# A layer norm's last step on VectorE instead of GpSimd, from period 8 of block 0 and in block 1's attention

## The chip, the cores and the metric

The kernel runs on one core of a Trainium2 chip. A core has five engines with a queue each: TensorE (PE in the profile: matrix products and transposes), VectorE (DVE), ScalarE (ACT), GpSimd (POOL) and SyncE (SP, which only starts transfers here). An engine executes its own queue strictly in the order in which it was written; between engines, semaphores order the work. The metric is the time of one execution on the device in microseconds (us). The number that a run is compared by is the median of several executions.

## The reference

There are 32 sequences of 256 tokens with 128 features, 8192 rows of 128 numbers in float32. Two blocks follow each other, each with an attention part and a part of experts.

```python
def _layer(x, ...):                       # block 0's attention part, run twice
    xl = _ln(x, ln1_g, ln1_b)
    q, k, v = ...                         # projections, rotary
    probs = softmax(q k / sqrt(64))
    x = x + att @ wo
    xl2 = _ln(x, ln2_g, ln2_b)
    hid = xl2 @ w1 + b1
    hid = hid * sigmoid(1.702 * hid)
    return x + hid @ w2

def _layernorm(x, axis=-1, eps=1e-05):
    m = jnp.mean(x, axis=axis, keepdims=True)
    v = jnp.var(x, axis=axis, keepdims=True)
    return (x - m) / jnp.sqrt(v + eps)
```

Block 0's experts: a router picks 8 of 64 experts for a token, each expert takes at most 64 tokens, and the weighted results are added to a shared expert's result. Block 1 has linear attention (with a layer norm of its output before the last projection) and 32 experts, one per token, again with a shared one. Layer norms without learned weights stand between the parts.

## The kernel before

**Tiles.** The 8192 rows are 64 tiles of 128 rows; four tiles make a group (`GT = 4`), so there are 16 groups of 512 rows. All rows live in `s_rows` on the chip. A layer norm always handles one group at a time, in `normed` (L103): for each of the four tiles VectorE computes mean and variance (`bn_stats` L109, `bn_aggr` L110, into `bn_mv`). GpSimd then makes 1/sqrt(variance + eps) for the four tiles in two small operations of 128x4, an addition (L111) and a power with −0.5 (L112), negates the mean (L118) and writes the four normalised tiles, `z = (x − mean) * rs`, with one 128x128 operation each (L120). In the form that block 1's attention uses (`on_act`), GpSimd multiplies the mean with the inverse deviation (L114) and VectorE writes the tiles (L116). `bn_mv` and `bn_rs` have three buffers, `z` four.

**Who uses the norm in block 0.** `norm_t` (L355) normalises a group into `z`, has TensorE transpose its four tiles (L127) and ScalarE copy the result to `xt` (L363). `project` (L366) does this ahead of the attention's projections, `second_norm` (L490) ahead of the hidden layer. `enter` (L186), the norm of the input rows, and `route` (L625), that between the blocks, call `normed` in the GpSimd form.

**Periods.** Block 0 runs in 18 periods, the loop at L583. A unit is a pair of groups in one of the two layers; there are 16. Period k runs attention for unit k (`softmax`, L391: scores L403, maxima L409, exponentials L418, transposes L435, products with the values L444, its result copied at L450) and, beside it (`beside`, L537), the second norms and hidden layer of unit k−1, the output layer of unit k−2 and the norms and projections of unit k+1. The hidden layer (`widen`, L476) has four steps a group: a matmul (L480), ScalarE's `m_z` from the result (L482, two buffers), ScalarE's tanh into `m_h` (L484, twelve buffers), and VectorE's product of both, again into `m_h` (L485), which sets the `m_z` buffer free. The output layer (`narrow`, L494) multiplies `m_h` at L498. Matmul results of most steps share two banks (`bank`, L73).

**The experts of block 0.** From period 8 on each period also runs two calls of `experts` (L295), each for four experts: two gathers of rows by index (L303), matmuls, and four scatter-adds of results into `moe0` in device memory (L341), so eight adds in a full period. Gathers and adds are indirect transfers, which GpSimd issues from its own queue. Every add waits for the one before it to have landed, since both add to the same array.

**Order.** The steps of a period are generators that `run` advances in turn. The framework's scheduler turns what they issue into one queue for each engine, before the kernel runs.

**Block 1.** `linear_attention` (L778) handles one group at a time and calls `normed` at L839 in the `on_act` form on `l_o`, in place; what it returns, the last GpSimd operation of the norm, is kept in `last_norm`, and the scatters in `send` (L763) are ordered behind it.

Of the kernel before, what the change touches and what calls it, by code (L numbers as in the profile page):

```python
# [16 lines left out]
F32 = mybir.dt.float32  # L17
# [8 lines left out]
P = 128  # L26
# [34 lines left out]
def recurrent_kernel(ctx: ExitStack, tc: tile.TileContext, x, consts, small0, wsd, wgu, wd, small1, bias1, wr, out):  # L61
# [38 lines left out]
    power = keep.tile([P, GT], F32, name="power")  # L100
    vec.memset(power, -0.5)

    def normed(wk, src, dst, on_act=False):  # L103

        st = wk.tile([P, GT, 6], F32, name="bn_st")
        mv = wk.tile([P, GT, 2], F32, name="bn_mv", bufs=3)
        rs = wk.tile([P, 2, GT], F32, name="bn_rs", bufs=3)
        for j in range(GT):
            vec.bn_stats(st[:, j], src[:, j])  # L109
            vec.bn_aggr(mv[:, j], st[:, j])  # L110
        pool.tensor_scalar(rs[:, 0], mv[:, :, 1], 1.0, EPS, ALU.mult, ALU.add)  # L111
        pool.tensor_tensor(rs[:, 0], rs[:, 0], power, ALU.pow)  # L112
        if on_act:
            ins = pool.tensor_tensor(rs[:, 1], mv[:, :, 0], rs[:, 0], ALU.mult)  # L114
            for j in range(GT):
                vec.tensor_scalar(dst[:, j], src[:, j], rs[:, 0, j : j + 1], rs[:, 1, j : j + 1], ALU.mult, ALU.subtract)  # L116
            return ins
        pool.tensor_scalar(rs[:, 1], mv[:, :, 0], -1.0, 0.0, ALU.mult, ALU.add)  # L118
        for j in range(GT):
            ins = pool.tensor_scalar(dst[:, j], src[:, j], rs[:, 1, j : j + 1], rs[:, 0, j : j + 1], ALU.add, ALU.mult)  # L120
        return ins

    def transposed(src):
# [10 lines left out]
    with ExitStack() as c0:  # L134
# [217 lines left out]
            order_of += [(p, 0), (p - 2, 1)]  # L352
        order_of += [(p, 1) for p in range(NG // 2 - 2, NG // 2)]

        def norm_t(g, copy):  # L355

            xs = s_all[:, g * GT : (g + 1) * GT]
            z = wk.tile([P, GT, D], F32, name="z", bufs=4)
            normed(wk, xs, z)
            yield  # L360
            ps = transposed(z)
            xt = wk.tile([P, GW], F32, tag="xt", name="xt", bufs=4)
            copy(xt, ps)  # L363
            yield xt

        def project(g, l, got):  # L366

            xt = None
            for xt in norm_t(g, act.copy):
                yield  # L370
            w = [par("attn", (4 * l + i) * D, D) for i in range(3)]
            qk = []
            for i, rot in enumerate(("rotq", "rotk")):
                ps = bank()
                pe.matmul(ps, w[i], xt, start=True, stop=True)  # L375
                t = wk.tile([P, GW], F32, name=f"a_qk{i}", bufs=4)
                vec.scalar_tensor_tensor(
                    t.rearrange("p (b s) -> p b s", s=SEQ), ps.rearrange("p (b s) -> p b s", s=SEQ),
                    fold[:, l, i : i + 1], bcast(const(rot), 1, 2), ALU.add, ALU.mult,
                )  # L380
                qk.append(t)
                yield
            ps = bank()
            for j in range(GT):
                pe.matmul(ps[:, j * D : (j + 1) * D], xt[:, j * P : (j + 1) * P], w[2], start=True, stop=True)
            v = wk.tile([P, GT, D], F32, name="a_v", bufs=4)
            act.copy(v, ps.rearrange("p (t d) -> p t d", d=D))
            got[g] = (qk, v)
            yield
# [97 lines left out]
                yield  # L487
            got[g] = hs

        def second_norm(g, got):  # L490
            for got[g] in norm_t(g, act.copy):
                yield

        def narrow(g, l, hs):  # L494
# [28 lines left out]
        def unit(k):  # L523
            p, l = order_of[k]
            return (2 * p, 2 * p + 1), l
# [3 lines left out]
        def first(g):  # L529
            yield from enter(g)  # L530
            if g == 0:
                fold_in()
            yield from project(g, 0, qkv)

        drain(run(*(first(g) for g in unit(0)[0])))

        def beside(k):  # L537

            if 1 <= k <= units:
                yield from run(*(second_norm(g, mid) for g in unit(k - 1)[0]))  # L540
            if 2 <= k:
                gs, l = unit(k - 2)
                yield from run(*(narrow(g, l, wide.pop(g)) for g in gs))
            if 1 <= k <= units:
                gs, l = unit(k - 1)
                yield from run(*(widen(mid.pop(g), l, wide, g) for g in gs))
            if k + 1 < units:
                gs, l = unit(k + 1)
                if gs[0] not in entered:
                    entered.update(gs)  # L550
                    yield from run(*(enter(g) for g in gs))
                yield from run(*(project(g, l, qkv) for g in gs))


        entered = {0, 1}
# [222 lines left out]
    def linear_attention(g):  # L778

        xt = xt_all[:, g * GW : (g + 1) * GW]  # L780
        ps = bank()
        pe.matmul(ps, par1("wq"), xt, start=True, stop=True)
        qf = wk.tile([P, GW], F32, name="l_q")
        act.activation(qf, ps, AF.Silu, bias=par1("bq"))
        q2 = wk.tile([P, GW], F32, name="l_q2", bufs=1)
        act.activation(q2, qf, AF.Square, bias=half)
        vec.tensor_scalar(qf, qf, 0.5, None, ALU.add)
        ps = bank()
        for j in range(GT):
            pe.matmul(ps[:, j * H1 : (j + 1) * H1], q2[:, j * P : (j + 1) * P], const("bones"), start=True, stop=True)  # L790
        norms = wk.tile([P, GT * (1 + O1) * H1], F32, name="l_n")
        qn, kn = norms[:, : GT * H1], norms[:, GT * H1 :]
        vec.tensor_copy(qn, ps[:, : GT * H1])
        yield

        kf = wk.tile([P, GT, O1 * D], F32, name="l_k")
        vf = wk.tile([P, GT, O1 * D], F32, name="l_v")
        for j in range(GT):
            ps = bank("sc", 4)
            pe.matmul(ps, xt[:, j * P : (j + 1) * P], par1("wkv"), start=True, stop=True)  # L800
            vec.tensor_tensor(kf[:, j], ps[:, : O1 * D], bias[:, : O1 * D], ALU.add)
            vec.tensor_tensor(vf[:, j], ps[:, O1 * D :], bias[:, O1 * D : 2 * O1 * D], ALU.add)
            if j % 2:
                yield

        sp.dma_start(xt.rearrange("p (t d) -> p t d", d=D), rows(moe1, g))
        act.activation(kf, kf, AF.Silu)
        k2 = wk.tile([P, GT * O1 * H1, D1], F32, tag="wide", name="l_k2")
        kflat = kf.rearrange("p t (h d) -> p (t h) d", d=D1)
        act.activation(k2, kflat, AF.Square, bias=half)  # L810
        vec.tensor_reduce(kn, k2, AX.X, ALU.add)
        yield
        act.activation(norms, norms, AF.Sqrt)
        vec.tensor_scalar(norms, norms, 1e-6, None, ALU.add)
        vec.reciprocal(norms, norms)  # L815
        vec.scalar_tensor_tensor(kflat, kflat, 0.5, bcast(kn, 2, D1), ALU.add, ALU.mult)
        yield
        ps = bank("tr", 2)
        for b in range(2):
            for k in range(O1):  # L820
                for j in range(2):
                    pe.matmul(  # L822
                        ps[:, (k * 2 + b) * D : (k * 2 + b + 1) * D], kf[:, 2 * b + j, k * D : (k + 1) * D],
                        vf[:, 2 * b + j, k * D : (k + 1) * D], start=j == 0, stop=j == 1,
                    )
        yield
        st4 = ps.rearrange("p (k b d) -> p k b d", b=2, d=D)
        st = wk.tile([P, 2, D], F32, name="l_st")
        vec.tensor_tensor(st, st4[:, 0], bcast(const("bmask"), 1, 2), ALU.mult)
        vec.tensor_tensor(st, st4[:, 1], st, ALU.mult)  # L830
        ps = bank()
        for j in range(GT):
            pe.matmul(ps[:, j * D : (j + 1) * D], qf[:, j * P : (j + 1) * P], st[:, j // 2], start=True, stop=True)
        o = wk.tile([P, GT, D], F32, tag="tok", name="l_o", bufs=3)
        vec.tensor_tensor(
            o.rearrange("p t (h d) -> p (t h) d", d=D1), ps.rearrange("p (n d) -> p n d", d=D1), bcast(qn, 2, D1), ALU.mult
        )
        yield
        last_norm.append(normed(wk, o, o, True))  # L839
        yield  # L840
        ps = transposed(o)
        ot = wk.tile([P, GW], F32, tag="chan", name="l_ot", bufs=3)
        act.activation(ot, ps, AF.Identity, bias=par1("lb"), scale=par1("lg"))
        yield
        ps = bank()
        for j in range(GT):
            pe.matmul(ps[:, j * D : (j + 1) * D], ot[:, j * P : (j + 1) * P], par1("wo"), start=True, stop=True)
        assert len(sent) >= (g + 1) * GT
        vec.tensor_tensor(
            s_all[:, g * GT : (g + 1) * GT], ps.rearrange("p (t d) -> p t d", d=D), bcast(bias[:, 4 * D :], 1, GT), ALU.add  # L850
        )
        yield
# [169 lines left out]
```

## Time and profile before

| what | value |
| --- | --- |
| median of 3 executions | 1429.88 us (1424.03 to 1430.29) |
| the profiled execution's own time | 1431.9 us |
| its span (first to last instruction) | 1430.1 us |
| mean clock granted to TensorE | 0.953 of full speed |
| `z` tiles written by GpSimd, 128x128 (L120) | 256, 504 ns each |
| `l_o` tiles written by VectorE, 128x128 (L116) | 64, 348 ns each |
| L111, L118, L114 on GpSimd, 128x4 | 237, 203, 200 ns each |

How to read the lines that follow: a group's line names the source line, engine, operation, the tile written and the tiles read, then how often it occurred, its busy time, the mean nanoseconds of one, and behind the last bar the idle time of the engine just before these instructions with what ended most of it. A line of the timeline has start and duration in us, engine, source line, operation and tiles, and in brackets a wait before it with what released it; neighbouring instructions of one kind can stand in one line. Durations and waits are of one profiled execution. Instructions that only issue a transfer are listed with the time that the issue took on GpSimd.

### The profile page before, as it was taken

To read this page: it belongs to the slowest core of one execution; us is meant where nothing else is said; L and a number is where in the kernel's file an instruction comes from. 1 tells how busy PE (TensorE), PEld (TensorE's weight loads), DVE (VectorE), ACT (ScalarE), POOL (GpSimd) and SP (SyncE) were. 2 spreads that over 40 slices of the span, in tenths; PEclk is the share of its full clock that TensorE was granted. 3 is DMA by queue.
4 is the path that set the end of the run, shared out by engine and by line. 5 is a ranking of instruction groups with operands and counts; after the bars stand their busy time and mean duration, and the time that the engine had idled before them with its cause. 6 is when DMAs were issued, how large, how long until landed. Compare 5 with 4: busy or idle time off the path is not lost. (4 is left out here: it accounts for less than half of the span.)

```text
span 1430.1 us, 22784 instructions
## 1 busy us (share of the span) xinstructions
PE 1250.7 (87%) x7395; PEld 871.3 (61%) x7395; DVE 920.6 (64%) x2971; ACT 773.1 (54%) x1842; POOL 683.4 (48%) x1100
## 2 busy tenths in 40 slices
PE   6989998899899999999999758899766899999787
PEld 4645665565567656766566435566444777788763
DVE  4689899869956565556454347755655565656437
ACT  1675566566666666566665434444333454645342
POOL 6353437442345665666645407652466444343430
PEclk9989999999999999999999988999787899999999
DMA  5022231210102212221220044211411467666656
GB/s 181 9 56 62 69 97 52 75 33 12 52 12 50 44 15 49 50 44 27 38 51 4 6 108 130 67 38 37 124 55 54 130 190 210 194 197 198 185 174 191
DMA packets 131079, 120.50 MB, mean 84 GB/s; under 512 B 17456, under 2 KB 108432, under 8 KB 130832
## 3 DMA queue, kind: packets, MB, share of 16 engines
q1 hardware_dynamic: 119184, 103.26, 24.8%
q0 software_dynamic: 11776, 15.78, 4.9%
q8 instruction: 59, 0.97, 0.3%
q14 instruction: 60, 0.49, 0.1%
HBM read 81.01 MB, written 37.99 MB: 83 GB/s over the span
## 5 line engine op out<-in xcount | busy, mean ns | idle before, releaser
L895 POOL DMA_INDIRECT back<-e_ys,e_toi x96 | 97.3, 1013 | 141.2 <-ACT e_ys L894 104.4
L418 ACT ACTIVATE a_pr<-ps_sc,a_nm 128x256 f32<-128x256 f32 x256 | 119.5, 480 | 74.5 <-DVE a_nm L409 69.0
L341 POOL DMA_INDIRECT moe<-e_y,sidx x64 | 95.1, 1486 | 128.4 <-DMA moe<-e_y,sidx 71.4
L480 PE MATMUL ps_mm<-xt,sw 128*128 128x512 f32 x256 | 134.5, 629 | 2.8 <-ACT r_ex L215 2.1
L111 POOL TENSOR_SCALAR bn_rs<-bn_mv 128x4 f32<-128x4 f32 x112 | 26.5, 237 | 220.5 <-DVE bn_mv L110 203.5
L120 POOL TENSOR_SCALAR z<-s_rows,bn_rs 128x128 f32<-128x128 f32 x256 | 125.8, 504 | 6.9
L498 PE MATMUL ps_mm<-sw,m_h 128*128 128x128 f32 x1024 | 126.5, 279 | 2.5 <-DVE s_h L250 0.9
L498 PEld LDWEIGHTS ps_mm<-sw,m_h 128*128 128x128 f32 x1024 | 118.5, 192 | 15.2 <-issue 8.2
L485 DVE SCALAR_TENSOR_TENSOR m_h<-m_h,m_z 128x512 f32<-128x512 f32 x128 | 88.2, 696 | 49.0 <-ACT m_h L484 48.4
L112 POOL TENSOR_TENSOR bn_rs<-bn_rs,power 128x4 f32<-128x4 f32 x112 | 114.4, 1022 | 1.3
L482 ACT ACTIVATE m_z<-ps_mm,fold 128x512 f32<-128x512 f32 x128 | 87.0, 688 | 43.8 <-PE ps_mm L480 43.5
L881 PE MATMUL ps_sc<-e_xt,e_w 128*128 128x128 f32 x768 | 101.2, 279 | 3.3 <-ACT e_xt L868 2.2
L409 DVE TENSOR_REDUCE a_nm<-ps_sc 128x2 f32<-128x512 f32 x128 | 83.1, 682 | 32.0 <-PE ps_sc L403 27.8
L881 PEld LDWEIGHTS ps_sc<-e_xt,e_w 128*128 128x128 f32 x768 | 94.7, 195 | 9.5 <-issue 5.8
L403 PE MATMUL ps_sc<-a_qk,a_qk 64*128 64x256 f32 x512 | 95.4, 412 | 1.4 <-ACT a_pr L418 1.2
L484 ACT ACTIVATE m_h<-m_z 128x512 f32<-128x512 f32 x128 | 80.2, 636 | 1.8
L435 PEld LDWEIGHTS ps_tr<-con,a_pr 128*128 128x128 f32 x512 | 59.0, 144 | 32.2 <-issue 20.3
L765 POOL DMA_INDIRECT xslot<-s_rows,dest x64 | 65.0, 1016 | 27.9 <-issue 18.5
L435 PE MATMUL ps_tr<-con,a_pr 128*128 128x128 f32 x512 | 75.1, 281 | 3.3 <-DVE key L236 2.2
L375 PE MATMUL ps_mm<-xt,sw 128*128 128x512 f32 x128 | 74.4, 693 | 3.9 <-ACT xt L363 1.6
L127 PEld LDWEIGHTS ps_tr<-con,z 128*128 128x128 f32 x256 | 33.0, 147 | 73.2 <-POOL z L120 45.5
L127 PE MATMUL ps_tr<-con,z 128*128 128x128 f32 x256 | 51.9, 298 | 28.9 <-POOL z L120 26.3
(225 smaller groups left out, 2982.0 us busy)
## 6 DMA issues: line engine op xcount, KB each, us to landing
e_w<-in_wr_dram SPq DMA_DIRECT2D x96, 384.0 KB
xslot<-zero SPq DMA_DIRECT2D x4, 1548.0 KB
e_x<-xslot SPq DMA_DIRECT2D x24, 258.0 KB
e_wg<-in_wgu_dram SPq DMA_DIRECT2D x16, 384.0 KB
x_in<-in_x_dram SPq DMA_DIRECT2D x16, 256.0 KB
tab<-s_rows SPq DMA_DIRECT2D x16, 256.0 KB
moe<-s_y SPq DMA_DIRECT2D x16, 256.0 KB
c_g<-moe SPq DMA_DIRECT2D x16, 256.0 KB
```

Of the source, the lines that this page charges most:

```text
L112: pool.tensor_tensor(rs[:, 0], rs[:, 0], power, ALU.pow)
L120: ins = pool.tensor_scalar(dst[:, j], src[:, j], rs[:, 1, j : j + 1], rs[:, 0, j : j + 1], ALU.add, ALU.mult)
L341: pool.indirect_dma_start(out=moe0, out_offset=bass.IndirectOffsetOnAxis(ap=sidx[:, 4 * q + e : 4 * q + e + 1], axis=0), in_=ye[:, e], in_ ...
L403: pe.matmul(sc[h][:, j * SEQ : (j + 1) * SEQ], qk[0][hd, q0 : q0 + P], qk[1][hd, b * SEQ : (b + 1) * SEQ], start=True, stop=True,)
L418: act.activation(pr[:, n], sc[h][:, j * SEQ : (j + 1) * SEQ], AF.Exp, bias=nm[:, n : n + 1], accum_out=su[:, n : n + 1],)
L435: pe.transpose(pts[:, n * P : (n + 1) * P], pr[:, n, k * P : (k + 1) * P], ident)
L480: pe.matmul(ps, par("w1", l * FF0 + f * P, P), xt, start=True, stop=True)
L482: act.activation(z, ps, AF.Identity, bias=fold[:, l, 3 + f : 4 + f])
L485: vec.scalar_tensor_tensor(h, h, 1.0, z, ALU.add, ALU.mult)
L498: pe.matmul(ps[:, j * D : (j + 1) * D], hs[f][:, j * P : (j + 1) * P], par("w2", l * FF0 + f * D, D), start=f == 0, stop=f == 3,)
L881: pe.matmul(ps[:, c * P : (c + 1) * P], wt[:, c * P : (c + 1) * P], xt[:, j * P : (j + 1) * P], start=True, stop=True,)
L895: ins = pool.indirect_dma_start(out=back, out_offset=bass.IndirectOffsetOnAxis(ap=toi[:, j : j + 1], axis=0), in_=ys[:, j], in_offset=None,)
```

## The change

`normed` takes the engine that is to write the tiles, `on`. With VectorE, GpSimd computes only the addition and the power, and VectorE writes the four tiles from the mean in `bn_mv` and the inverse deviation in `bn_rs`. That form is used in block 0 by `first` (the two groups ahead of the periods) and, from period 8 on, by the second norms and projections in `beside`; in block 1 by the attention's norm. Periods 0 to 7, `enter` and `route` keep GpSimd's form. The inverse deviation and the negated mean have a tile each, `bn_rs` and `bn_nm`. A form for ScalarE is in the code and is not called.

```diff
-    def normed(wk, src, dst, on_act=False):
+    def normed(wk, src, dst, on=None):
...
-        rs = wk.tile([P, 2, GT], F32, name="bn_rs", bufs=3)
+        rs = wk.tile([P, GT], F32, name="bn_rs", bufs=3)
         for j in range(GT):
             vec.bn_stats(st[:, j], src[:, j])
             vec.bn_aggr(mv[:, j], st[:, j])
-        pool.tensor_scalar(rs[:, 0], mv[:, :, 1], 1.0, EPS, ALU.mult, ALU.add)
-        pool.tensor_tensor(rs[:, 0], rs[:, 0], power, ALU.pow)
-        if on_act:
-            ins = pool.tensor_tensor(rs[:, 1], mv[:, :, 0], rs[:, 0], ALU.mult)
+        pool.tensor_scalar(rs, mv[:, :, 1], 1.0, EPS, ALU.mult, ALU.add)
+        ins = pool.tensor_tensor(rs, rs, power, ALU.pow)
+        if on is vec:
             for j in range(GT):
-                vec.tensor_scalar(dst[:, j], src[:, j], rs[:, 0, j : j + 1], rs[:, 1, j : j + 1], ALU.mult, ALU.subtract)
+                vec.tensor_scalar(dst[:, j], src[:, j], mv[:, j, 0:1], rs[:, j : j + 1], ALU.subtract, ALU.mult)
             return ins
-        pool.tensor_scalar(rs[:, 1], mv[:, :, 0], -1.0, 0.0, ALU.mult, ALU.add)
-        for j in range(GT):
-            ins = pool.tensor_scalar(dst[:, j], src[:, j], rs[:, 1, j : j + 1], rs[:, 0, j : j + 1], ALU.add, ALU.mult)
+        nm = wk.tile([P, GT], F32, name="bn_nm", bufs=3)
+        pool.tensor_scalar(nm, mv[:, :, 0], -1.0, 0.0, ALU.mult, ALU.add)
...
+        for j in range(GT):
+            ins = pool.tensor_scalar(dst[:, j], src[:, j], nm[:, j : j + 1], rs[:, j : j + 1], ALU.add, ALU.mult)
         return ins
...
-            yield from project(g, 0, qkv)
+            yield from project(g, 0, qkv, vec)
...
         def beside(k):
 
+            on = pool if k < 8 else vec
             if 1 <= k <= units:
-                yield from run(*(second_norm(g, mid) for g in unit(k - 1)[0]))
+                yield from run(*(second_norm(g, mid, on) for g in unit(k - 1)[0]))
...
-                yield from run(*(project(g, l, qkv) for g in gs))
+                yield from run(*(project(g, l, qkv, on) for g in gs))
...
-        last_norm.append(normed(wk, o, o, True))
+        last_norm.append(normed(wk, o, o, vec))
```

In the changed kernel line numbers are 5 higher behind the changed function, and 6 higher behind the first lines of `beside`; the new writes on VectorE are at L115.

More of the change, by code (lines that the diff above doesn't have):

```diff
@@ L110, in normed @@
             vec.bn_aggr(mv[:, j], st[:, j])
-        pool.tensor_scalar(rs[:, 0], mv[:, :, 1], 1.0, EPS, ALU.mult, ALU.add)
-        pool.tensor_tensor(rs[:, 0], rs[:, 0], power, ALU.pow)
-        if on_act:
-            ins = pool.tensor_tensor(rs[:, 1], mv[:, :, 0], rs[:, 0], ALU.mult)
+        pool.tensor_scalar(rs, mv[:, :, 1], 1.0, EPS, ALU.mult, ALU.add)
+        ins = pool.tensor_tensor(rs, rs, power, ALU.pow)
+        if on is vec:
             for j in range(GT):
-                vec.tensor_scalar(dst[:, j], src[:, j], rs[:, 0, j : j + 1], rs[:, 1, j : j + 1], ALU.mult, ALU.subtract)
+                vec.tensor_scalar(dst[:, j], src[:, j], mv[:, j, 0:1], rs[:, j : j + 1], ALU.subtract, ALU.mult)
             return ins
-        pool.tensor_scalar(rs[:, 1], mv[:, :, 0], -1.0, 0.0, ALU.mult, ALU.add)
+        nm = wk.tile([P, GT], F32, name="bn_nm", bufs=3)
+        pool.tensor_scalar(nm, mv[:, :, 0], -1.0, 0.0, ALU.mult, ALU.add)
+        if on is act:
+            pool.tensor_tensor(nm, nm, rs, ALU.mult)
+            for j in range(GT):
+                act.activation(dst[:, j], src[:, j], AF.Identity, scale=rs[:, j : j + 1], bias=nm[:, j : j + 1])
+            return ins
         for j in range(GT):
-            ins = pool.tensor_scalar(dst[:, j], src[:, j], rs[:, 1, j : j + 1], rs[:, 0, j : j + 1], ALU.add, ALU.mult)
+            ins = pool.tensor_scalar(dst[:, j], src[:, j], nm[:, j : j + 1], rs[:, j : j + 1], ALU.add, ALU.mult)
         return ins
@@ L353, in recurrent_kernel, with norm_t @@
         order_of += [(p, 1) for p in range(NG // 2 - 2, NG // 2)]
-        def norm_t(g, copy):
+        def norm_t(g, copy, on):
             xs = s_all[:, g * GT : (g + 1) * GT]
             z = wk.tile([P, GT, D], F32, name="z", bufs=4)
-            normed(wk, xs, z)
+            normed(wk, xs, z, on)
             yield
@@ L364, in norm_t, with project @@
             yield xt
-        def project(g, l, got):
+        def project(g, l, got, on):
             xt = None
-            for xt in norm_t(g, act.copy):
+            for xt in norm_t(g, act.copy, on):
                 yield
@@ L488, in widen, with second_norm @@
             got[g] = hs
-        def second_norm(g, got):
-            for got[g] in norm_t(g, act.copy):
+        def second_norm(g, got, on):
+            for got[g] in norm_t(g, act.copy, on):
                 yield
```

## The prediction

> **What bounds the kernel now.** I read the page's table of engines, then its costliest groups, then only the stretch that the change touches: the eight periods from 446 to 824 us in which the experts' results are added (P1 to P8, each from its first scatter-add to the next period's; starts 446.38, 491.64, 539.53, 587.70, 634.65, 679.92, 727.74, 778.32). From the page:
>
> ```profile
> PE 1250.7 (87%) x7395; PEld 871.3 (61%) x7395; DVE 920.6 (64%) x2971; ACT 773.1 (54%) x1842; POOL 683.4 (48%) x1100
> ...
> L341 POOL DMA_INDIRECT moe<-e_y,sidx x64 | 95.1, 1486 | 128.4 <-DMA moe<-e_y,sidx 71.4
> ...
> L120 POOL TENSOR_SCALAR z<-s_rows,bn_rs 128x128 f32<-128x128 f32 x256 | 125.8, 504 | 6.9
> ...
> L112 POOL TENSOR_TENSOR bn_rs<-bn_rs,power 128x4 f32<-128x4 f32 x112 | 114.4, 1022 | 1.3
> ```
>
> TensorE is the bound, GpSimd far from one. Busy time by windows, P3 and P5 (PE, PEld, DVE, ACT, POOL, clock, DMA share, GB/s):
>
> ```profile
> 539.50:587.70 48.20, 45.07 (x286) 30.32 (x288) 27.34 (x81) 30.03 (x79) 29.20 (x41) 0.96 0.20 41
> 634.70:679.90 45.20, 43.37 (x286) 29.62 (x286) 27.44 (x81) 29.90 (x79) 29.25 (x40) 1.00 0.21 42
> ```
>
> TensorE works for 94 to 96% of a period, VectorE and GpSimd for 57 to 65%. So what counts is who holds TensorE up, and in which order GpSimd's and VectorE's queues stand. The timeline of P3:
>
> ```profile
> 556.43 0.30 DVE L110 BATCH_NORM_AGGREGATE bn_mv<-bn_st 128x2 f32<-128x6 f32 x2
> ...
> 556.98 0.69 DVE L485 SCALAR_TENSOR_TENSOR m_h<-m_h,m_z 128x512 f32<-128x512 f32 x1 [0.25 <-ACT m_h L484]
> ...
> 559.84 1.29 ACT L482 ACTIVATE m_z<-ps_mm,fold 128x512 f32<-128x512 f32 x2
> ...
> 560.60 1.08 PE L444 MATMUL ps_mm<-a_pt,a_v 128*64 128x256 f32 x8
> ...
> 563.28 1.40 POOL L341 DMA_INDIRECT moe<-e_y,sidx  x1 [1.79 <-DMA moe<-e_y,sidx]
> ...
> 566.48 1.83 POOL L341 DMA_INDIRECT moe<-e_y,sidx  x1 [1.80 <-DMA moe<-e_y,sidx]
> ...
> 568.38 0.19 POOL L111 TENSOR_SCALAR bn_rs<-bn_mv 128x4 f32<-128x4 f32 x1
> 568.66 0.19 POOL L118 TENSOR_SCALAR bn_rs<-bn_mv 128x4 f32<-128x4 f32 x1
> 568.81 1.04 POOL L112 TENSOR_TENSOR bn_rs<-bn_rs,power 128x4 f32<-128x4 f32 x1
> ...
> 569.96 1.75 POOL L120 TENSOR_SCALAR z<-s_rows,bn_rs 128x128 f32<-128x128 f32 x4
> ...
> 570.47 1.77 PE L127 MATMUL ps_tr<-con,z 128*128 128x128 f32 x4 [2.55 <-POOL z L120]
> ```
>
> To be seen: VectorE has the statistics of the unit's first second norm (call it A; B is its other group, C and D the two groups that project next) at 556.7, but GpSimd starts A at 568.4, because eight scatter-adds stand ahead of it, one every 3.3 us (1.45 to issue, 1.8 for the previous add to land). Nobody but TensorE's transposes needs A, and they lose only 2.55 us; meanwhile VectorE goes on with the hidden activations m_h.
>
> **What the Trainium skill says.** "GPSIMD Engine Reference", § 4.1 Engine selection, gives elementwise work to VectorE. The trace agrees by less than that page's factor two: 504 ns for a 128x128 tile at L120, 348 ns at L116. "TensorE: Matmul & The Clock Gate", Part 1, has TensorE's clock fall after an idle window of about 3.4 us. The trace agrees: after a wait of 7.58 us in P8 eight L444 matmuls take 1.98 us where they take 1.08 in P3. "DMA: Bandwidth & Descriptors", Rules for kernel authors, says that an accumulating DMA has to wait for the earlier one on the same bytes; the 1.8 us at each L341 is that wait, so the chain of adds will not get faster.
>
> **The change part by part.** Off GpSimd: 34 groups lose L118 and four L120 (34 x (0.20 + 4 x 0.504) = 75 us), 16 lose L114 (3 us). Onto VectorE: 34 x 4 writes of 0.348 = 47 us, of which 5.5 in each full period. GpSimd was no bound; the direct gain is only where TensorE waits for z.
>
> *Gain, P1 to P6.* The transposes of A wait for GpSimd's z: 0.85 + 0.53 us in P1, P4 and P5, which with slower transposes (0.77 + 0.76 where an undisturbed four take 0.60) makes 2.3; in P2, P3, P6 2.25, 2.55 and 2.35, transposes 1.1 slower, and about 1.4 of slow matmuls behind, 4.9. All gone: 3 x 2.3 + 3 x 4.9 = 21.6. The periods bear it out: P3 is 3.0 us longer than P5.
>
> *Loss, P1 to P6.* In the order of the changed kernel the queues in such a period stand thus. GpSimd: seven adds (with four gathers between), power of A, eighth add, powers of B, C, D. VectorE: statistics of A, four z of A, then the m_h. Nothing stands between A's last bn_aggr and its first z. VectorE takes its queue in order, so it stands from A's statistics (17.2 us after the period's start) until the power of A: the end of add seven, less 1.0 (one pair of gathers moves behind), plus 1.4 (L111, L112 and gaps). Behind it stand m_h. m_z has two buffers, so the third m_z, 20.3 us after the period's start (559.84 in P3), waits for the first m_h, and with it ScalarE, the two matmul banks, and TensorE's next L444. The third m_z comes at: end of add seven + 0.4 + 0.34 (first z's lead) + 0.69 (one m_h), and add seven ends 23.4, 24.7, 25.1, 23.7, 23.2, 25.2 us after the start. With the remaining three z counted in part, it is late by 4.6, 5.9, 6.4, 4.9, 4.4, 6.4: together 32.6 us. TensorE has nothing else, as its own queue is in order too. Stalls of this length slow what follows: L444 1.98 for 1.08 and L480 1.65 to 1.93 for 1.12 make 1.4 to 1.7 a period where nothing absorbs them; I take 1.4 x 6 = 8.5.
>
> *VectorE's own pace.* 5.5 us of z a period and the waits of B, C, D for a power (1.3 us each less the small operations ahead of them). The work alone is 33 us over six periods, and VectorE has some 20 us free in each, but m_h and the softmax reductions (L409) are what ScalarE waits for. From zero (all in idle time) to 27; I take 14.
>
> *P7.* Six adds stand ahead of the first power (C's, 749.8 now), VectorE reaches it near 741: blocked 9, with slow matmuls behind 11. The stalls that go are 3.01 + 0.85 + 0.53 with slow matmuls behind, 7.3. Net +4. *P8.* All eight adds come first and TensorE already waits 7.58 us there; z comes at most 1.2 earlier: −1. *Block 1.* The wait of L116 for L114 (14.7 us over all) loses a 0.2 us operation 11 times or so: −2. The scatters of block 1 (L765) are ordered behind a group's last GpSimd norm operation, now the power instead of L114: the same place in the queue, nothing. *The two groups ahead of the periods*: eight z written faster by 0.15: −1.
>
> Sum: 32.6 + 8.5 − 21.6 + 14 + 4 − 1 − 2 − 1 = **+33.5 us**. The profiled execution took 1431.9 us with a span of 1430.1; the median, 1429.88, is 0.2 below that span, so I add to the median: **1463**.
>
> **The rivals.** *Faster: the block is not met.* If the power of A were there when VectorE asks, the gains stand alone: 21.6 + 7.3 (P7) + 1 + 2 + 1 = 33, less some pacing, say 5: 1402. For it: before, the same stall cost TensorE little. Against: the adds would have to end some 7 us earlier; it decides at 2.2 us an add instead of 3.3, or if anything but m_h stood behind z. *Even: blocked, but absorbed.* If half of the delay were taken up by buffers (the score banks hold softmax work that needs no m_h) and the pacing were nothing: (32.6 + 8.5) / 2 − 21.6 + 4 − 4 = −1; with some pacing 1429 to 1440. For it: GpSimd's A was 2.55 us late for TensorE, not 8. Against: the third m_z stands on ScalarE's queue ahead of the attention output (L450) and the copies of the next transposes, so all of them wait. *Much slower*: pacing at its 27, restart of slow matmuls at 1.7, B and C adding 1 us a period: 33.5 + 13 + 2 + 6 = +54.5: 1484. For it: bn_aggr and z of B, C, D follow each other with little between; against: 20 us of idle VectorE a period. That the change is not built as it reads is excluded: 136 z stand on VectorE's queue and are gone from GpSimd's.
>
> **How the numbers follow.** Forecast (1445 to 1475): 0.50; much slower: 0.22; even: 0.15; faster: 0.13. Two executions of this kernel differ by up to 0.4%, so under 0.5% (7 us) is no change. Faster by more: all of the faster case and a little of the even one, 0.14. Within: 0.07. Slower: 0.79. The range of 1422 to 1494 leaves out most of the faster case and the far end of the slow one.
>
> **What would show it.** Right: a wait of VectorE at the new z (L115) for the power of L112 of some 6 to 9 us in P1 to P7, 45 to 65 in all; TensorE waiting for ScalarE's m_z at L444 or L480 instead of for z at L127; full periods of 49 to 54 us; GpSimd's busy time down by 78, VectorE's up by 47 us. Wrong: full periods under 46 us with short waits at L115 (faster), or long waits at L115 while TensorE stays above 94% busy (even). A change far from 446 to 824 us would mean that I looked in the wrong place.

## The result and the profile after

The changed kernel takes 1464.57 us (median of 4 executions, 1459.96 to 1471.28) against 1427.01 for the kernel before: a ratio of 1.026, with a 95% interval from 1.0224 to 1.0295. It is slower by 37.6 us; the forecast was 33.5. The profiled execution of the changed kernel took 1459.96 us with a span of 1458.2. It is the fastest of its four executions, while the profiled one of the kernel before, 1431.9 us, is slower than that kernel's median; so the two traces lie only 28.1 us apart.

From the page of the changed kernel, the table of engines and three groups (line numbers are 5 or 6 higher than before):

```profile
PE 1253.0 (86%) x7395; PEld 872.7 (60%) x7395; DVE 949.9 (65%) x3107; ACT 775.0 (53%) x1842; POOL 608.0 (42%) x914
...
L346 POOL DMA_INDIRECT moe<-e_y,sidx x64 | 95.7, 1495 | 130.1 <-DMA moe<-e_y,sidx 62.6
...
L112 POOL TENSOR_TENSOR bn_rs<-bn_rs,power 128x4 f32<-128x4 f32 x112 | 114.1, 1019 | 4.2
...
L115 DVE TENSOR_SCALAR z<-s_rows,bn_mv,bn_rs 128x128 f32<-128x128 f32 x136 | 41.9, 350 | 84.9 <-POOL bn_rs L112 84.8
```

GpSimd lost 75 us of work and VectorE gained 29, with 350 ns for each z where GpSimd needed 504 (neighbouring operations of VectorE overlap, so that four z in a row take 1.12 us). Yet in front of the new z VectorE stood idle for 84.9 us, nearly all of it for the power of L112. The waits between 430 and 870 us (total, number of times, longest), one line of the kernel before, then those of the changed kernel:

```profile
PE ps_tr L127 <- POOL z L120: 25.3, 14, 7.6
...
DVE z L115 <- POOL bn_rs L112: 82.4, 30, 9.5
...
ACT m_z L487 <- DVE m_h L490: 45.3, 13, 8.4
...
PE ps_mm L449 <- ACT m_z L487: 33.3, 6, 6.9
...
PE ps_tr L440 <- DVE a_pr L432: 11.7, 7, 7.0
...
PE ps_tr L132 <- DVE z L115: 8.5, 2, 7.3
```

The lines form a chain: VectorE waits for GpSimd, ScalarE for VectorE, TensorE for ScalarE, six times. The wait of TensorE for z at the transposes, 25.3 us in this stretch before, is gone but for the 8.5 us in two places, both in P8. The same chain in P3, from the timeline of the changed kernel (VectorE has the statistics of A, the first group of the unit's second norms, at 570.1):

```profile
569.85 0.30 DVE L110 BATCH_NORM_AGGREGATE bn_mv<-bn_st 128x2 f32<-128x6 f32 x2
...
576.33 1.40 POOL L346 DMA_INDIRECT moe<-e_y,sidx  x1 [2.73 <-DMA moe<-e_y,sidx]
...
577.79 0.20 POOL L111 TENSOR_SCALAR bn_rs<-bn_mv 128x4 f32<-128x4 f32 x1
578.07 1.04 POOL L112 TENSOR_TENSOR bn_rs<-bn_rs,power 128x4 f32<-128x4 f32 x1
579.15 0.35 DVE L115 TENSOR_SCALAR z<-s_rows,bn_mv,bn_rs 128x128 f32<-128x128 f32 x1 [9.00 <-POOL bn_rs L112]
579.41 0.68 DVE L490 SCALAR_TENSOR_TENSOR m_h<-m_h,m_z 128x512 f32<-128x512 f32 x1
...
580.19 0.69 ACT L487 ACTIVATE m_z<-ps_mm,fold 128x512 f32<-128x512 f32 x1 [6.80 <-DVE m_h L490]
...
580.93 1.97 PE L449 MATMUL ps_mm<-a_pt,a_v 128*64 128x256 f32 x8 [6.94 <-ACT m_z L487]
```

Read it from the bottom up. TensorE's products with the values begin 6.94 us late, because ScalarE has not emptied a bank into m_z; that was 6.80 us late, because both m_z buffers were full until VectorE's first m_h; VectorE stood 9.00 us at z, whose power came after the seventh add. Then the matmuls run slowly, 1.97 us where eight of them took 1.08 before.

Busy time by windows, P3 and P5 of the changed kernel (PE, PEld, DVE, ACT, POOL, clock, DMA share, GB/s):

```profile
553.50:607.50 54.00, 45.19 (x286) 30.66 (x286) 30.79 (x97) 30.27 (x79) 20.66 (x21) 0.91 0.18 35
...
659.10:710.80 51.70, 44.25 (x286) 29.85 (x286) 30.84 (x96) 30.24 (x79) 20.84 (x20) 0.93 0.19 37
```

TensorE's share of these periods fell from 94 and 96% to 84 and 86%. By the starts of the adds in the two traces the span grows by 28.1 us: 2.7 up to the first add, 35.8 from the first add to the last (356.8 to 392.6), −1.7 between there and block 1's first scatter, and −8.7 from that scatter to the end.

### The profile page after: what moved, and what is told of

Read it like the earlier page. It is cut to its first block, busy times and chain, and to the rows that moved or that the text cites. A ratio compares the mean times of both kernels' runs of the same rounds, so it can differ in the third digit from the quotient of the medians.

```text
span 1458.2 us, 22658 instructions
## 1 busy us (share of the span) xinstructions
PE 1253.0 (86%) x7395; PEld 872.7 (60%) x7395; DVE 949.9 (65%) x3107; ACT 775.0 (53%) x1842; POOL 608.0 (42%) x914
## 3 DMA queue, kind: packets, MB, share of 16 engines
q1 hardware_dynamic: 119184, 103.26, 24.4%
## 4 chain that ended last, share of the span: by engine, by line
PE 44%; DVE 21%; POOL 12%; issue 8%; DMA 8%; ACT 6%; another core or an unknown queue 0%; SPq 0%; POOLq 0%; ACTq 0%; DVEq 0%
DMA moe<-e_y,sidx 4%; PE ps_mm L485 4%; PE ps_mm L503 4%; POOL bn_rs L112 3%; PE ps_mm L449 3%; PE ps_mm L380 3%; PE ps_tr L132 3%; PE ps_sc L806 3%; POOL moe L346 3%; PE ps_sc L887 2%; PE ps_mm L896 2%; PE ps_tr L440 2%; DMA e_x<-xslot 2%; PE ps_sc L408 2%; DVE m_h L490 2%
## 5 line engine op out<-in xcount | busy, mean ns | idle before, releaser
L485 PE MATMUL ps_mm<-xt,sw 128*128 128x512 f32 x256 | 140.2, 653 | 2.8 <-ACT r_ex L220 2.1
L112 POOL TENSOR_TENSOR bn_rs<-bn_rs,power 128x4 f32<-128x4 f32 x112 | 114.1, 1019 | 4.2
L449 PE MATMUL ps_mm<-a_pt,a_v 128*64 128x256 f32 x512 | 78.7, 430 | 39.9 <-ACT m_z L487 33.3
L115 DVE TENSOR_SCALAR z<-s_rows,bn_mv,bn_rs 128x128 f32<-128x128 f32 x136 | 41.9, 350 | 84.9 <-POOL bn_rs L112 84.8
L408 PE MATMUL ps_sc<-a_qk,a_qk 64*128 64x256 f32 x512 | 91.2, 412 | 1.4 <-ACT a_pr L423 1.2
L380 PE MATMUL ps_mm<-xt,sw 128*128 128x512 f32 x128 | 72.3, 663 | 8.8 <-DVE a_qk L382 5.5
L441 ACT COPY a_pt<-ps_tr 128x512 f32<-128x512 f32 x128 | 71.1, 589 | 14.1 <-PE ps_tr L440 13.6
L449 PEld LDWEIGHTS ps_mm<-a_pt,a_v 128*64 128x64 f32 x512 | 34.1, 148 | 71.0 <-ACT m_z L487 36.6
```

The source lines that it names most:

```text
L112: ins = pool.tensor_tensor(rs, rs, power, ALU.pow)
L408: pe.matmul(sc[h][:, j * SEQ : (j + 1) * SEQ], qk[0][hd, q0 : q0 + P], qk[1][hd, b * SEQ : (b + 1) * SEQ], start=True, stop=True,)
L449: pe.matmul(av[h * DPH : (h + 1) * DPH, :SEQ], v[:, 2 * b + k, h * DPH : (h + 1) * DPH], pt[:, k, h], start=k == 0, stop=k == 1,)
L485: pe.matmul(ps, par("w1", l * FF0 + f * P, P), xt, start=True, stop=True)
```

## The experiments

The runs came from several chips, on which the kernel before took 1413 to 1425 us. So each is compared by its ratio to the kernel before on the same chip; us over before are that ratio's.

**VectorE works out the inverse deviation itself.** All else as in the changed kernel, from period 8 on. The small constant added to the variance is left out there, and the root is approximated:

```diff
+        if on == "own":
+            y = wk.tile([P, GT], F32, name="bn_y", bufs=2)
+            v = mv[:, :, 1]
+            vec.tensor_scalar(rs.bitcast(I32), v.bitcast(I32), 1, None, ALU.logical_shift_right)
+            vec.tensor_scalar(rs.bitcast(I32), rs.bitcast(I32), -1.0, float(0x5F3759DF), ALU.mult, ALU.add)
+            for _ in range(2):
+                vec.tensor_tensor(y, rs, rs, ALU.mult)
+                vec.scalar_tensor_tensor(y, y, -0.5, v, ALU.mult, ALU.mult)
+                vec.scalar_tensor_tensor(rs, y, 1.5, rs, ALU.add, ALU.mult)
+            for j in range(GT):
+                ins = vec.tensor_scalar(dst[:, j], src[:, j], mv[:, j, 0:1], rs[:, j : j + 1], ALU.subtract, ALU.mult)
+            return ins
...
-            on = pool if k < 8 else vec
+            on = pool if k < 8 else "own"
```

> From period 8 on VectorE works out the inverse deviation itself (an estimate from the float's bits and two Newton steps, eight operations of 128x4), so that no z there waits for GpSimd; the rest is as in the changed kernel. Theory (z waits for a power that stands behind the scatter-adds): VectorE's stand of 82 us at the new z is gone, the full periods fall from about 52 us to 45 to 46, the time to 1390 to 1412 us. Rival (the work of z on VectorE costs the time): VectorE gets more work still, the full periods stay over 50 us and the time over 1455. Rival (half and half): 1425 to 1440.

Measured: 1383.02 us, ratio 0.969 (0.9637 to 0.9744), 44 us under the kernel before. Busy time by windows, its first full period and P3 (columns as above):

```profile
448.40:491.70 43.30, 43.01 (x286) 30.05 (x284) 33.95 (x129) 29.88 (x79) 15.96 (x13) 1.00 0.22 44
...
535.00:578.60 43.60, 42.95 (x285) 30.05 (x284) 33.98 (x129) 29.94 (x79) 15.61 (x13) 1.00 0.22 43
```

TensorE works for 99% of the period at its full clock, although VectorE has more to do than before or in the changed kernel: 34 us of 43.3. The adds do not come earlier: the seventh of P1 ends 24.4 us after the period's start, in the changed kernel 22.0; only VectorE no longer waits for what stands behind them. So it is the wait for GpSimd that costs, not the work of z. The run also shows how long a period is without a stall: 43.3 us. The time is 7 us below the expected range, and the ratio is the lowest of all runs.

**The power later by two powers.**

```diff
+        if on == "late":
+            lag = wk.tile([P, GT], F32, name="bn_lag", bufs=1)
+            pool.tensor_tensor(lag, mv[:, :, 1], power, ALU.pow)
+            pool.tensor_tensor(lag, lag, power, ALU.pow)
+            on = vec
...
-                yield from run(*(second_norm(g, mid, on) for g in unit(k - 1)[0]))
+                yield from run(*(second_norm(g, mid, "late" if on is vec and g % 2 == 0 else on) for g in unit(k - 1)[0]))
```

> The changed kernel with two more powers of 1.0 us each (results not used) on GpSimd ahead of the first second norm of each unit from period 8 on. Theory: the power of A comes 2.1 us later, VectorE stands that much longer and TensorE with it: 8 x 2.1 = 17 us, 1478 to 1485 us. Rival (GpSimd's lateness is absorbed by buffers, VectorE's work is what costs): 0 to 4 us, 1462 to 1470.

Measured: 1482.61 us, ratio 1.0378 (1.0322 to 1.0434), 17 us over the changed kernel on the same scale. Its waits from 430 to 900 us:

```profile
DVE z L120 <- POOL bn_rs L117: 101.4, 26, 11.6
ACT m_z L492 <- DVE m_h L495: 64.0, 14, 10.6
...
PE ps_mm L454 <- ACT m_z L492: 48.6, 6, 9.1
```

In P3 the power ends 2.0 us later behind add seven than in the changed kernel (3.4 us for 1.4). The longest wait of VectorE grew by 2.1 us and that of TensorE by 2.2; TensorE's six waits grew from 33.3 to 48.6 us, 2.55 each. What GpSimd is late by, TensorE is late by: nothing between them absorbs it.

**A alone behind the adds; C and D alone behind them.** In own_cd the projections use VectorE's own root and the second norms wait for GpSimd; in own_ab it is the other way round.

```diff
-                yield from run(*(project(g, l, qkv, on) for g in gs))
+                yield from run(*(project(g, l, qkv, "own" if on is vec else on) for g in gs))
```

> The projections (C and D) take the inverse deviation from VectorE, as in own_root; the second norms (A and B) wait for GpSimd's power as in the changed kernel. Here all eight adds stand ahead of A's power, in the changed kernel seven. Theory (A's stand behind the adds is most of the loss): about 7 periods with TensorE held up 8 to 9 us and 1.5 us of slow matmuls behind, on top of own_root's 1383: 1440 to 1462 us. Rival (the loss comes from many short waits for a power, or from VectorE's work): 1385 to 1410.

> The mirror of own_cd: second norms take the inverse deviation from VectorE, the projections wait for GpSimd's power, which comes after the eight adds when these are done, but for P7. Theory: no stand of VectorE over 2 us but in P7 (about 9, 10 to 12 us of time), and of the rest the two waits of 1.0 to 1.4 us for a power, which in project_vec held up an expert's copy on ScalarE by 2.4 us a period with slow matmuls behind: 1400 to 1425 us. Rival (a wait of 1.4 us on VectorE is absorbed): 1383 to 1396.

Measured: own_cd 1467.16 us, ratio 1.0384 (1.0341 to 1.0428); own_ab 1377.30 us, ratio 0.9753 (0.9712 to 0.9794). In own_cd the waits between 430 and 850 us have the chain again (VectorE at z, ScalarE at m_z):

```profile
DVE z L127 <- POOL bn_rs L124: 73.5, 15, 10.6
...
ACT m_z L499 <- DVE m_h L502: 58.8, 7, 9.9
...
PE ps_mm L497 <- ACT m_z L499: 56.0, 7, 9.5
```

with full periods of 55 to 58 us by the starts of the adds. All eight adds stand ahead of A here, one more than in the changed kernel, so the run shows that A's wait alone is enough for a loss of this size, and not which share of the changed kernel's loss is A's. TensorE's 56.0 us for m_z are what was expected; the time is some 18 us past the range by the ratio, since TensorE lost a further 13.6 us at L461 to the copies of the experts' results, which had come late as well. In own_ab the waits of VectorE from 440 to 800 us have one entry of weight:

```profile
DVE z L127 <- POOL bn_rs L124: 11.4, 7, 8.9
```

that of P7, where C stands behind six adds: 8.93 us, and P7 takes 55.0 us where it took 43.3 in own_root. Of the other six, five last 0.25 us and one 1.20, and P1 to P6 take 43.0 to 43.2 us each. The time, 1390 us by the ratio, is in the rival's range, but whether a wait of 1.0 to 1.4 us for a power is absorbed was hardly tested, since P1 to P6 have no such wait. What the pair shows is that a wait behind the adds costs its whole length and more, and that where there is none nothing is lost.

**Second norms left to GpSimd, projections on VectorE.**

```diff
-                yield from run(*(second_norm(g, mid, on) for g in unit(k - 1)[0]))
+                yield from run(*(second_norm(g, mid, pool) for g in unit(k - 1)[0]))
```

> The changed kernel with the second norms (A and B) left on GpSimd from period 8 on; VectorE writes z only ahead of the projections (C and D). Theory: A's stand of VectorE is gone but for period P7, where C stands behind six adds (about 4 us); TensorE's own stalls at the z of A come back. 1420 to 1434 us, full periods of 46 to 49 us. Rival (VectorE's work costs): half of the work, so half of the loss: 1440 to 1450.

Measured: 1461.82 us, ratio 1.0239 (1.0176 to 1.0302), not to be told from the changed kernel: a miss, and beyond the rival's range too. The timeline of this run around the norms of C and D in P3:

```profile
590.44 1.12 DVE L115 TENSOR_SCALAR z<-s_rows,bn_mv,bn_rs 128x128 f32<-128x128 f32 x4 [0.97 <-POOL bn_rs L112]
...
593.52 0.35 DVE L115 TENSOR_SCALAR z<-s_rows,bn_mv,bn_rs 128x128 f32<-128x128 f32 x1 [1.41 <-POOL bn_rs L112]
593.78 1.28 DVE L414 TENSOR_REDUCE a_nm<-ps_sc 128x2 f32<-128x512 f32 x2
594.51 0.47 ACT L423 ACTIVATE a_pr<-ps_sc,a_nm 128x256 f32<-128x256 f32 x1 [3.12 <-DVE a_nm L414]
...
596.32 0.38 ACT L317 COPY e_xg<-ps_tr 128x256 f32<-128x256 f32 x1
...
596.75 1.54 PE L322 MATMUL ps_mm<-e_xg,e_wg 128*96 128x64 f32 x8 [2.37 <-ACT e_xg L317]
```

The same kind of chain in another place: VectorE's maxima stand behind a z that waits for its power, ScalarE's exponentials behind the maxima, the experts' copy behind the exponentials. It costs TensorE 2.4 us in each of P1 to P5, in P2 and P3 on top of A's old stall of 2.2. P1 to P7 take 355.7 us, 24 more than before. Of these, 12 are TensorE's busy time, for the same matmuls: the clock was 0.88 in P3 and 0.86 in P4. In P7, where C stands behind six adds, TensorE waits 7.5 and 1.8 us, and the period takes 55.6 us for 50.6. So A's wait for the adds is not the only one that can reach TensorE. In the changed kernel the norms of C and D wait 0.97 and 0.15 us, and this stall is not there; whether it is the longer second wait or the other order of the queues that brings it about, these runs do not separate.

**Three m_z buffers.**

```diff
-            z = wk.tile([P, GW], F32, name="m_z", bufs=2)
+            z = wk.tile([P, GW], F32, name="m_z", bufs=3)
...
-            h = wk.tile([P, GW], F32, name="m_h", bufs=12)
+            h = wk.tile([P, GW], F32, name="m_h", bufs=11)
```

> The changed kernel with three m_z buffers for two, paid with eleven m_h for twelve. Theory (the stand of VectorE reaches TensorE through the third m_z, which waits for the first m_h): the wait moves to the fourth m_z, TensorE goes on for one more matmul and what it lets through, 1 to 2.5 us a period: 1448 to 1460 us, and VectorE stands at the new z as long as before. Rival (TensorE is held up by z itself): no change, 1462 to 1468.

Measured: 1473.31 us, ratio 1.0322 (1.0266 to 1.0377): slower, a miss. TensorE's wait in P3 does shrink from 6.94 us to 3.64, and P1 to P4 take 51.0, 51.8, 51.1 and 51.0 us against 52.2, 52.2, 54.0 and 51.6: gains of 0.4 to 3.0 where 1 to 2.5 were expected. But the first add comes 5.9 us later, and P5 to P7 lose again what was won; that the other numbers of buffers change the order of the queues is the likely reason, and not shown. As a test of the whole time it is void; as one of the place it fits.

**z written twice.** own_root with every z of these periods written a second time.

```diff
-            for j in range(GT):
+            for j in [*range(GT), *range(GT)]:
```

> own_root with every z of the periods from 8 on written twice by VectorE: 5.5 us of VectorE more in a period of 43.3, of which it worked 34. If the work of z is hidden as long as nothing waits (the forecast's 14 us for VectorE's pace were wrong as work): the periods stay under 44 us, 0 to 5 us over own_root, a ratio to before of 0.967 to 0.974. If VectorE's work does reach TensorE (the forecast's term, 14 us for 5.5 us a period): 10 to 25 us over own_root, 0.976 to 0.988.

Measured: 1381.72 us, ratio 0.9718 (0.9678 to 0.9759). Its window for the first full period:

```profile
446.60:490.00 43.40, 43.11 (x286) 30.06 (x285) 38.60 (x145) 29.98 (x79) 16.24 (x13) 1.00 0.22 44
```

VectorE has 38.6 us of 43.4, and the period is 0.1 us longer than in own_root. P1 to P7 sum to 305.4 us against 303.0, nearly all of the difference in P7. The work of z is all but free here, where nothing stands still; behind a stall it was not tested.

**The parts apart.** la_only has the new form in block 1's attention alone; periods_only in the periods alone.

```diff
-            on = pool if k < 8 else vec
+            on = pool
```

> Only block 1's attention norm in the new form, block 0 as before. What the changed kernel gains from the start of block 1's attention to the end, 8.7 us by the two traces, is the form's own: 1411 to 1420 us. Rival (the gain of the forecast, 2 us, and the rest from how block 0 ended): 1421 to 1427.

> Only the periods from 8 on in the new form; the two groups ahead of them and block 1's attention norm in the old one. If the attention's norm is worth 8.7 us: 1467 to 1478 us, with the end of block 0 37 us later than before. Rival (2 us): 1462 to 1466.

Measured: la_only ratio 0.9971 (0.9956 to 0.9986), 4 us gained; periods_only 1.0268 (1.0224 to 1.0312), 38 us lost, not to be told from the changed kernel's 1.026. The periods are the whole loss. By their ratios la_only stands at 1423 us and periods_only at 1465, both in the range of the rival, the forecast's 2 us for the attention; the interval of la_only allows 2 to 6. Of the 8.7 us in the trace some 4 are confirmed.

**Further on VectorE.** own_root with block 1's attention norm, and then also the norm between the blocks, in the same form.

```diff
-        last_norm.append(normed(wk, o, o, vec))
+        last_norm.append(normed(wk, o, o, "own"))
...
-        normed(wk, x_all[:, tl], xn)
+        normed(wk, x_all[:, tl], xn, "own")
```

> own_root, and block 1's attention norm takes its inverse deviation from VectorE too (eight operations of 128x4 there instead of an addition and a power on GpSimd with two hops). TensorE waits for l_o there 16.6 us in the kernel before; if the hops are more than half of it: 3 to 10 us under own_root, a ratio of 0.962 to 0.967. If VectorE's eight operations cost as much as the hops: the same as own_root.

> own_la, and the norm between the blocks on VectorE as well, z and inverse deviation. TensorE waits for c_xn of GpSimd 23 us there, so up to 15 us are to be had, but VectorE has the choosing of experts in the same stretch: ratio 0.950 to 0.968. Rival: VectorE becomes the bound of that stretch, 5 to 10 us over own_la.

Measured: own_la ratio 1.000 (0.9981 to 1.0018), own_la_route 1.0018 (0.9996 to 1.004): both miss, and lose all that own_root won. Block 0 is as fast as in own_root; the loss lies in block 1. The scatters start their last transfer early (1045.8 us in own_la, 1070.0 in own_root), but the first expert result returns at 1126.7 instead of 1084.5, after a single wait of 35.7 us on VectorE, which ends at 1054.9, after the last scatter, and whose releaser the profile doesn't name. The scatters are ordered behind the last norm operation, which is now one of VectorE's. Why this delays the experts wasn't followed further and stays open.

## Why the prediction was right

*The signs.* The forecast named waits of 6 to 9 us at L115 in P1 to P7, 45 to 65 us in all. The seven long ones measure 6.8, 7.8, 9.0, 7.0, 7.6, 7.5 and 8.8: 54.4. TensorE waits at L449, as named, and full periods take 50.7 to 54.0 us, P7 55.3. One sign was off: VectorE's busy time rose by 29 us and not by 47, in part since neighbouring operations overlap in the trace.

*A's stand, P1 to P6.* The forecast had TensorE late by 4.6, 5.9, 6.4, 4.9, 4.4, 6.4, in all 32.6 us. TensorE's waits for m_z measure 4.7, 5.7, 6.9, 4.9, 5.6, 5.4: 33.3. The queue order and the one add every 3.3 us were enough for this.

*The gain.* The forecast had 21.6 + 7.3 = 28.9 us for TensorE's old stalls in P1 to P7. The seven periods took 331.9 us before and 303.0 in own_root, where nothing stalls: 28.9. One period was put in the wrong class: P4, with 2.3 expected, gave 3.5.

*Slow matmuls.* 8.5 us, and 2 in P7, were forecast. TensorE's busy time over P1 to P7 is 314.20 us in the changed kernel and 300.55 in own_root: 13.7.

*P7.* 9 us of waiting were forecast, 7.0 + 1.8 came, where C's z holds up the softmax:

```profile
784.54 0.66 PE L440 MATMUL ps_tr<-con,a_pr 128*128 128x128 f32 x2 [6.97 <-DVE a_pr L432]
...
787.03 1.98 PE L449 MATMUL ps_mm<-a_pt,a_v 128*64 128x256 f32 x8 [1.82 <-DVE s_rows L468]
```

*VectorE's pace, the term that was wrong in kind.* "From zero (all in idle time) to 27; I take 14." The work itself costs next to nothing, as own_root and own_twice show. TensorE's idle time in the seven periods is 53.6 us, in own_root 2.5. Without these 2.5 and the 33.3 and 8.8 above, 9.0 us are left, in short waits of 0.4 to 0.8 us (a_pr, a_qk, and others). So the term of 14 was 9, and what was left is waits, not work.

*The small ones.* The forecast had −1 for the groups ahead of the periods: the first add is 2.7 us later. It had −1 for P8: TensorE's longest wait for z there fell from 7.58 to 7.34 us, and P8 is 0.1 shorter by its adds. It had −2 for block 1: −4 by la_only, −8.7 in the trace.

The terms as measured for P1 to P7 are 33.3 + 8.8 + 9.0 + 13.7 − 28.9 = 35.9. That they meet the 35.9 by which these periods grew checks nothing, since the 9.0 is what was left over. The forecast's for the same stretch were 32.6 + 8.5 − 21.6 + 14 + 4 = 37.5: the mechanism and the large terms were right, the pace was 5 too high, the slow matmuls 3 too low. Outside this stretch luck had a part. In the traces the start was 3.7 us worse than forecast and the rest better, block 1 alone by 6.7, which makes 28.1 us in all; the 37.6 of the medians lies on the other side of the 33.5.

The faster rival was built on the right point, the power being there when VectorE asks: own_root makes it so, and lands at 0.969, where the rival's 1402 would be 0.98. It took 5 us off for pacing, and left out P8, where TensorE waited 9.6 us for z before and not at all in own_root.

## What to carry to other kernels

Moving work from a slow engine to a faster one moves its place in a queue too: ask which input it waits for and what that producer has in its queue ahead of it. The same lateness costs differently by who waits. In P3 before, the z of A were started 13.2 us after their statistics were ready, and TensorE, which alone wanted them, lost 2.55 us; in the changed kernel VectorE stood for 9.00 us, and since ScalarE and TensorE need its other results, TensorE lost 6.94. In this kernel the large operation moved alone lost 2.6%, and the small one moved with it won 3.1%. A third way, the power placed ahead of the adds in GpSimd's own queue, was not tried.

## What had not been expected of the hardware

For a group, eight operations of 128x4 and four z on VectorE (own_root) beat an addition and a power on GpSimd, 1.3 us together, and the same four z by 81 us over the kernel, by ratio.

TensorE's clock fell after shorter waits than the 3.4 us that the prediction names. In project_vec no wait of TensorE in P1 to P6 is longer than 2.4 us. In its P4 TensorE stood idle for 3.0 us of 51.8 in all, yet the mean clock was 0.86, and the matmuls took 48.8 us where they took 43.1 in own_root's P4. The length of the waits alone doesn't settle it: P2 of that run, with 2.4 and 2.2, had 0.93, and before, P1 and P4 with the same waits of at most 0.9 had 1.00 and 0.96.
